# Macaron block on one core: KAN sums on four strips of the array instead of two, with another order of the start

## The chip, the cores and the metric

One core of a Trainium2 chip runs the whole program; the other cores are idle. The metric is the device time of one execution in microseconds, as the median of several runs. Shorter is better.

## The reference

Sixteen sequences (rows, below) of 512 tokens with 128 features pass through six residual steps; the first three concern the change.

```python
x = x + 0.5 * _L0_ffn_ref(_layernorm(x, axis=-1), ...)   # the KAN
x = x + _L0_attn_ref(_layernorm(x, axis=-1), ...)        # causal attention, 16 heads of 8, 4 key heads, RoPE
x = x + 0.5 * _L0_ffn_ref(_layernorm(x, axis=-1), ...)   # the same KAN again
x = x + 0.5 * _L1_ffn_ref(...)                           # 8 experts, each takes its best 128 tokens of a row
x = x + _L1_attn_ref(...)                                # gated linear recurrence
x = x + 0.5 * _L1_ffn_ref(...)                           # the experts again
```

The KAN maps 128 features to 64 scalars, gives each scalar 16 hidden ReLU units of its own, sums them with weights to 64 scalars again, and maps these to 128 features:

```python
s = jnp.einsum('btd,dm->btm', x, Win) + bin_         # 64 scalars
h = jax.nn.relu(s[..., None] * W1 + b1)              # 64 x 16
g = jnp.einsum('btmh,mh->btm', h, W2) + b2           # 64
out = jnp.einsum('btm,md->btd', g, Wout) + bout
```

## The kernel before, in words

All 16 rows of x stay in SBUF (`x[b]`, 128 x 4 x 128). The program is written as Python generators. Each runs one small piece of work up to a `yield`; `turn()` steps every open generator once, first those in `urgent`, then those in `sides`. What stands in the instruction queues of the engines is the order in which these pieces were stepped when the program was built. Nothing reorders it on the chip, apart from the waits.

**Rows.** From the main loop at the end, each row of attention takes 44 turns. In a turn `weights(b)` (L590 on) makes one bank of transposed scores on PE (L608, 72 + 27 = 99 partitions of `kp` and `qp`, bf16), its exponential on ACT (L611, into `pt`) and the causal mask of the diagonal block on POOL (L613). In the same turn `maxima(b + 1)` makes one bank of scores of the next row on PE (L550; a mask through L546) and its maximum on DVE (L555, L560). Both kinds of banks are double-buffered in PSUM. After a quarter of a row, `outputs` multiplies `pt` with the values (L631, four heads on four 32-column strips), transposes (L642) and divides (L646, L647). `max_rows` turns half a row's maxima into extra rows of `qp` (L581 transposes, L585 copies into `mr`, then DMAs on SP).

**Side work.** During rows from b = 0 on a budget per turn (`MOST`: pe 1.5, dve 1.15, act 0.85, pool 1.45) spreads the other work: a generator that says `yield from need(pe=1.0)` waits for a turn with that much room. The side work is: `norm` (L257 and L261 statistics on DVE, L263 and L264 on POOL, L278 on DVE, transposes L288 on PE, copy L292 on ACT); `kan(b)`, twice per row, before and after attention; `attn_in(b)`, the projections and rotation of a later row; `stage_out`, `gated`, `routing`.

**kan(b).** One fp32 matmul (L303) makes the 64 scalars twice, on partitions 0 to 63 and 64 to 127; ACT copies them to `kan_s` (L307). `kan_held` lets one KAN at a time use the accumulator `ps_kg`. Then, over 15 turns, ACT makes eight activations (L329), each with two hidden units per scalar, into four rotating buffers `kan_h`. After every second one, a pair of matmuls (L335, 128 x 64 weights `w2d`, 512 columns) adds to `ps_kg`: the first into partitions 0 to 63, the second into 64 to 127. ACT copies the sum (L340), PE applies `wout` (L346, doubled over both halves), DVE adds to x (L349). A constant is added to x on POOL (L332).

**attn_in(b).** The rotated queries `ta` and keys `ka` are split into three bf16 parts by `parts`: cast on ACT (L356), subtract on POOL (L359), cast on ACT (L362), subtract on POOL (L365). `spread` writes each part to DRAM on SP's queue, from where DMAs load `kp` (L434) and `qp` (L442) with the parts repeated.

**The start.** Constants are loaded on ACT's queue (L123 to L134) and SP's (L147 on), x on SP's. `center_win` folds the mean into `win`. Row 0's first pieces are stepped, then `prepare()` (L457 on: `rbias`, `kcst`, `w2d`, folded `wq`, `wk`, `wv`, masks, memsets of ten `QP` on POOL at L493 and of three `KP` on DVE at L495 and L496, `gateT`), with row 0 after it in each turn. Then rows 1 and 2. Row 0's maxima fill 44 turns of their own before the paced rows. After the rows comes the expert stage with the recurrence.

Of the kernel before, what the change touches and what calls it, by code (L numbers as in the profile page):

```python
# [8 lines left out]
F32 = mybir.dt.float32  # L9
# [7 lines left out]
P = 128  # L17
S = 512
NT = S // P
D = 128  # L20
M = 64
HALF = 8
HD = 8
# [21 lines left out]
def tile_macaron(  # L45
# [51 lines left out]
    with ExitStack() as ph:  # L97
# [4 lines left out]
        vap = ph.enter_context(tc.tile_pool(name="p1_va", bufs=4))  # L102
        hp = ph.enter_context(tc.tile_pool(name="p1_h", bufs=4))
        ptp = ph.enter_context(tc.tile_pool(name="p1_pt", bufs=2))
# [12 lines left out]
        nc.vector.tensor_scalar_add(center, ident, -1.0 / D)  # L117
        win = cst.tile([D, 2, M], F32, name="win")
        binc = cst.tile([P, 1], F32, name="binc")
        kw1 = cst.tile([P, HALF], F32, name="kw1")  # L120
        kb1 = cst.tile([P, HALF], F32, name="kb1")
        kw2 = cst.tile([P, HALF], F32, name="kw2")
        nc.scalar.dma_start(out=win, in_=win_in.unsqueeze(1).to_broadcast([D, 2, M]))  # L123
        nc.scalar.dma_start(out=kw1, in_=kw1_in.rearrange("m (a h) -> a m h", a=2))
        nc.scalar.dma_start(out=binc, in_=bin_in.unsqueeze(0).to_broadcast([2, M]))
        nc.scalar.dma_start(out=kb1, in_=kb1_in.rearrange("m (a h) -> a m h", a=2))
        nc.scalar.dma_start(out=kw2, in_=kw2_in.rearrange("m (a h) -> a m h", a=2))
        kb2 = cst.tile([M, 1], F32, name="kb2")
        nc.scalar.dma_start(out=kb2, in_=kb2_in.unsqueeze(1))
        wout = cst.tile([P, D], F32, name="wout")  # L130
        nc.scalar.dma_start(out=wout, in_=wout_in.unsqueeze(0).to_broadcast([2, M, D]))
        bout = cst.tile([1, D], F32, name="bout")
        nc.scalar.dma_start(out=bout, in_=bout_in.unsqueeze(0))
        nc.scalar.dma_start(out=gate_sb, in_=gate_in)  # L134
        rbias = cst.tile([P, HALF], F32, name="rbias")

        w2d = cst.tile([P, HALF, M], F32, name="w2d")
        eye2 = cst.tile([P, M], F32, name="eye2")
        ones = cst.tile([1, P], F32, name="ones1")
# [14 lines left out]
        rope = cst.tile([P, 2, S], F32, name="rope")  # L154
        nc.sync.dma_start(out=rope, in_=rope_in)
        for b in range(1, B):
            load(b)
# [64 lines left out]
        def bank(shape, dtype, name, work=0.0):  # L222


            while held[0] == 2 or (paced[0] and work > room["pe"]):
                yield
            room["pe"] -= work
            held[0] += 1
            return mm.tile(shape, dtype, name=name, tag="mm")

        def freed():
            held[0] -= 1
# [66 lines left out]
        def kan(b):  # L299

            _, xT = yield from norm(x[b])
            ps = yield from bank([P, S], F32, "ps_s", 0.9)
            nc.tensor.matmul(ps, lhsT=win.rearrange("d a m -> d (a m)"), rhs=xT, start=True, stop=True)  # L303
            yield
            sk = w2p.tile([P, S], F32, name="kan_s")
            take(act=0.6)
            nc.scalar.copy(sk, ps)  # L307
            freed()
            yield
            while kan_held[0]:  # L310
                yield
            kan_held[0] = 1

            pg = kap.tile([P, S], F32, name="ps_kg")
            hs = []
            begin = now[0]
            for t in range(HALF + 1):
                while now[0] < begin + 15 * t // 8:
                    yield
                pair = t % 2 == 0 and t > 0  # L320
                work = {"act": 0.8} if t < HALF else {}
                if pair:
                    work["pe"] = 1.0
                if t == 1:
                    work["pool"] = 1.25
                yield from need(**work)
                if t < HALF:
                    h = hp.tile([P, S], F32, name="kan_h")
                    nc.scalar.activation(h, sk, AF.Relu, bias=rbias[:, t : t + 1], scale=kw1[:, t : t + 1])  # L329
                    hs.append(h)  # L330
                if t == 1:
                    nc.gpsimd.tensor_tensor(x[b], x[b], kcst.unsqueeze(1).to_broadcast([P, NT, D]), ALU.add)  # L332
                if pair:
                    for i in range(2):
                        nc.tensor.matmul(pg[i * M : (i + 1) * M, :], lhsT=w2d[:, t - 2 + i, :], rhs=hs[t - 2 + i],  # L335
                                         start=(t == 2), stop=(t == HALF))
                yield
            gT = hp.tile([P, S], F32, name="kan_h")
            take(act=0.6)
            nc.scalar.copy(gT, pg)  # L340
            kan_held[0] = 0
            kans[0] -= 1
            yield
            po = yield from bank([P, NT, D], F32, "ps_ko", 0.9)
            for c in range(NT):
                nc.tensor.matmul(po[:, c, :], lhsT=gT[:, bass.ts(c, P)], rhs=wout, start=True, stop=True)  # L346
            yield
            take(dve=0.7)
            nc.vector.tensor_add(x[b], po, x[b])  # L349
            freed()  # L350
            yield

        def parts(r, dst, copies, **work):

            yield from need(**work)
            copies(dst[:, 0, :], r)  # L356
            yield
            yield from need(pool=1.15)
            nc.gpsimd.tensor_tensor(r, r, dst[:, 0, :], ALU.subtract)  # L359
            yield  # L360
            yield from need(**work)
            copies(dst[:, 1, :], r)  # L362
            yield
            yield from need(pool=1.3)
            nc.gpsimd.tensor_tensor(dst[:, 2, :], r, dst[:, 1, :], ALU.subtract)  # L365
            yield
# [8 lines left out]
        def attn_in(b, st):  # L375
# [45 lines left out]
            def keys():  # L421
                yield from need(pool=1.25)
                nc.gpsimd.tensor_tensor(ka, ka, kb, ALU.add)
                yield
                yield from parts(ka, kpart, nc.scalar.copy, act=0.6)

# [25 lines left out]
        def center_win():  # L452
            psc = yield from bank([P, 2 * M], F32, "ps_kc0")
            centered(psc, win.rearrange("d a m -> d (a m)"))
            freed()

        def prepare():  # L457

            nc.vector.scalar_tensor_tensor(rbias, in0=kw1, scalar=binc, in1=kb1, op0=ALU.mult, op1=ALU.add)
            nc.gpsimd.memset(ones, 1.0)  # L460
            nc.gpsimd.memset(onec, 1.0)
            psc = yield from bank([1, D], F32, "ps_kc")
            nc.tensor.matmul(psc, lhsT=kb2, rhs=wout[0:M, :], start=True, stop=True)
            nc.vector.tensor_add(kcr, psc, bout)
            freed()
            yield

# [3 lines left out]
            freed()  # L471
            nc.vector.tensor_add(eye2, ident[:, 0:M], ident[:, M:P])
            for u in range(HALF):
                nc.vector.tensor_scalar(w2d[:, u, :], eye2, kw2[:, u : u + 1], 0.5, ALU.mult, ALU.mult)
                if u == HALF // 2:
                    yield
            yield
# [9 lines left out]
            nc.vector.tensor_copy(wk[:, 1, :, hh:HD], wk[:, 0, :, 0:hh])  # L487
            make_identity(nc, identb)
            nc.gpsimd.memset(causal[:, 0 : S - P], 0.0)
            make_causal_mask(nc, own, NEG)  # L490
            yield
            for i in range(NQP):
                nc.gpsimd.memset(QP[i][MXR - 32 : MXR, :, :], 0.0)  # L493
                if i < NKP:
                    nc.vector.memset(KP[i][MXR - 32 : MXR, :, :], 0.0)  # L495
                    nc.vector.memset(KP[i][MXR : MXR + 3, :, :], 1.0)  # L496
                yield
            psg = yield from bank([D, E], F32, "ps_gate")
            nc.tensor.transpose(psg, gate_sb, ident[0:E, 0:E])
            nc.vector.tensor_copy(gateT, psg)  # L500
            freed()
            yield

# [60 lines left out]
        def max_rows(b, half, maxs):  # L564
# [17 lines left out]
            yield  # L582
            mr = w2p.tile([3 * H2, S], BF16, name="mr")
            take(dve=0.4)
# [337 lines left out]
        def folded():  # L922


            tmp = w2p.tile([P, 2, M, 4], F32, name="wu", tag="kan_s")
            wu, wvb = tmp[:, 0, :, :], tmp[:, 1, :, :]
# [40 lines left out]
        def recurrence(pair):  # L967
# [8 lines left out]
            yield  # L976
            fg = w2p.tile([P, S], F32, name="fg", tag="kan_s")
            nc.scalar.activation(fg, pf, AF.Tanh, scale=0.5)
# [58 lines left out]
        def finish(*gs):  # L1037
# [3 lines left out]
            paced[0] = pace  # L1041

        run(center_win())
        first = stage_in(0, sts[0])
        for _ in range(8):
            step(first)
        sides.append(prepare())
        sides.append(first)
        for _ in range(12):
            turn()  # L1050
# [98 lines left out]
```

## Time and profile before

| what | value |
|---|---|
| median of 3 runs | 1758.36 us (1757.0 to 1758.48) |
| profiled execution, its own time | 1763.15 us |
| its span | 1761.4 us |
| mean granted PE clock | 0.968 |
| PE busy | 1636.1 us (93%) |
| DVE busy | 1106.0 us (63%) |
| ACT busy | 996.6 us (57%) |
| POOL busy | 996.6 us (57%) |
| stages by time | start to 76 us, row 0's maxima to 128 us, rows to about 1010 us, experts to the end |

A line of a timeline has its start in us, its length in us, the engine, the line of the kernel, the operation, what it writes and reads, partitions and elements, the count, and in brackets how long the engine sat idle before it and what ended that. PEld are weight loads, which run beside matmuls. An fp32 matmul leaves two records. A wait line reads: who waited, for whom, us in total, times, longest.

### The profile page before, as it was taken

The page shows a single profiled execution, that of the slowest core. Times are in us where ns is not written, and L with a number is a line of the kernel's source. Part 1 is how long each engine was busy: PE and PEld are TensorE (multiplying, and loading weights), DVE is VectorE, ACT ScalarE, POOL GpSimd, SP SyncE. Part 2 cuts the span into 40 slices and gives each one's busy share as a digit, 9 for nine tenths or more (in the row PEclk, how much of TensorE's full clock was granted, in tenths as well). Part 3 has the DMA queues.
Part 4 walks back from the last instruction along what each step waited for, and adds up shares of the span by engine and source line. Part 5 has one row for each costly group of instructions (what it writes and reads, how often), then busy time and mean ns, then how long its engine had stood idle before and what let it go on. Part 6 is the DMA issues. An engine that isn't in the chain of part 4 may idle for free. (4 is left out here: it accounts for less than half of the span.)

```text
span 1761.4 us, 35249 instructions
## 1 busy us (share of the span) xinstructions
PE 1636.1 (93%) x12879; PEld 1110.9 (63%) x12879; DVE 1106.0 (63%) x3594; ACT 996.6 (57%) x2000; POOL 996.6 (57%) x1463
## 2 busy tenths in 40 slices
PE   3688999999999999999989899999999999999996
PEld 2234444444444454444444389799988889999996
DVE  5477767777777788878877137734458444672222
ACT  2435667787777776776666654344443334444443
POOL 5524445455554555455434767577663677647773
PEclk8879989999999999999999899999998999999998
DMA  4110111011101111011022113233322233323342
GB/s 116 57 66 26 50 47 30 35 48 54 42 31 40 51 54 38 21 50 50 25 71 68 32 43 70 49 73 65 66 59 45 58 67 71 68 52 69 65 81 47
DMA packets 101753, 94.77 MB, mean 54 GB/s; under 512 B 11859, under 2 KB 90140, under 8 KB 101340
## 3 DMA queue, kind: packets, MB, share of 16 engines
q1 hardware_dynamic: 74512, 67.45, 12.4%
q0 software_dynamic: 26048, 24.93, 8.8%
q8 instruction: 101, 1.65, 0.4%
q14 instruction: 72, 0.59, 0.1%
q10 hardware_dynamic: 1020, 0.15, 0.0%
HBM read 58.93 MB, written 37.49 MB: 55 GB/s over the span
## 5 line engine op out<-in xcount | busy, mean ns | idle before, releaser
L611 ACT ACTIVATE pt<-ps_st 128x512 f32<-128x512 f32 (+1 forms) x704 | 386.9, 561 | 242.3 <-PE ps_st L608 236.9
L613 POOL TENSOR_SCALAR_AFFINE_SELECT pt<-pt 128x128 f32<-128x128 f32 (+2 forms) x704 | 246.9, 355 | 409.1 <-ACT pt L611 404.3
L555 DVE CUSTOM_DVE_ANT_0 below<-ps_sc,causal 128x512 bf16<-128x512 f32 (+1 forms) x512 | 316.3, 618 | 120.8 <-PE ps_sc L550 106.6
L867 ACT ACTIVATE mo<-ps_h 128x512 f32<-128x512 f32 x256 | 153.1, 598 | 260.9 <-PE ps_h L865 260.7
L791 POOL DMA_INDIRECT xg<-xnd,tokI x256 | 250.1, 977 | 79.4 <-issue 42.8
L865 PE MATMUL ps_h<-xin,mw 128*128 128x128 f32 x2048 | 279.2, 279 | 0.0
L880 PE MATMUL ps_y<-mw,mo 128*128 128x128 f32 x2048 | 273.7, 277 | 0.0
L550 PE MATMUL ps_sc<-kp,qp 72*128 72x512 bf16 (+3 forms) x1024 | 261.4, 308 | 10.2 <-DVE maxs L555 7.5
L608 PE MATMUL ps_st<-qp,kp 99*128 99x512 bf16 (+3 forms) x1024 | 261.0, 308 | 5.6 <-ACT pt L611 4.6
L912 POOL DMA_INDIRECT sum<-ye,tokI x124 | 201.8, 1628 | 100.9 <-issue 25.3
L865 PEld LDWEIGHTS ps_h<-xin,mw 128*128 128x128 f32 x2048 | 250.5, 192 | 6.4 <-issue 3.7
L880 PEld LDWEIGHTS ps_y<-mw,mo 128*128 128x128 f32 x2048 | 251.0, 193 | 2.2 <-issue 0.8
L608 PEld LDWEIGHTS <-kp 99*128 99x128 bf16 x1024 | 94.3, 101 | 204.5 <-issue 186.3
L329 ACT ACTIVATE kan_h<-kan_s,rbias,kw 128x512 f32<-128x512 f32 x256 | 206.5, 814 | 7.6 <-PE ps_kg L335 7.3
L560 DVE TENSOR_REDUCE maxs<-ps_sc 128x2 f32<-128x512 f32 (+1 forms) x192 | 130.5, 685 | 69.2 <-PE ps_sc L550 68.2
L631 PE MATMUL ps_av<-pt,va 128*32 128x512 f32 (+3 forms) x2048 | 166.8, 444 | 0.0
L335 PE MATMUL ps_kg<-kan_h,w2d 128*64 128x512 f32 x512 | 164.2, 639 | 2.2 <-ACT kan_h L329 2.2
L550 PEld LDWEIGHTS <-qp 72*128 72x128 bf16 x1024 | 97.6, 101 | 56.0 <-issue 33.8
L886 DVE TENSOR_TENSOR mo<-mo 128x128 bf16<-128x128 f32 x132 | 38.9, 295 | 137.7 <-ACT mo L871 137.5
L898 PE MATMUL acc<-mo 128*128 128x128 bf16 x1584 | 112.4, 219 | 6.3 <-DVE mo L886 6.2
L898 PEld LDWEIGHTS <-mo 128*128 128x128 bf16 x1584 | 98.9, 98 | 24.1 <-issue 22.9
L631 PEld LDWEIGHTS ps_av<-pt,va 128*32 128x32 f32 x2048 | 53.6, 109 | 92.7 <-issue 49.1
(195 smaller groups left out, 2333.3 us busy)
## 6 DMA issues: line engine op xcount, KB each, us to landing
qp<-qs SPq DMA_DIRECT2D x64, 288.0 KB
xnd<-kan_x SPq DMA_DIRECT2D x32, 256.0 KB
sum<-x SPq DMA_DIRECT2D x31, 256.0 KB
qs<-qpart SPq DMA_DIRECT2D x48, 128.0 KB
kp<-ks SPq DMA_DIRECT2D x48, 96.0 KB
x<-in_L_attn_x_dram SPq DMA_DIRECT2D x16, 256.0 KB
mw<-in_L_ffn_w_dram SPq DMA_DIRECT2D x16, 256.0 KB
xg<-xnd,tokI POOLq DMA_INDIRECT x256, 2.5
```

The lines of the kernel that those rows point to most:

```text
L329: nc.scalar.activation(h, sk, AF.Relu, bias=rbias[:, t : t + 1], scale=kw1[:, t : t + 1])
L550: nc.tensor.matmul(v[:, u, 0:n], lhsT=qp[r][0 : 9 * HD, g, bass.ts(c, P)], rhs=kp[0 : 9 * HD, r, 0:n], start=alone, stop=(u == len(gs) - 1 ...
L555: nc.vector.tensor_tensor_reduce(below[:, 0:n], v[:, 0, 0:n], causal[:, S - n : S], 1.0, LOWEST, ALU.add, ALU.max, accum_out=maxs[:, c, h ...
L608: nc.tensor.matmul(v[:, u, 0:n], lhsT=kp[ROWS, r, bass.ts(c, P)], rhs=qp[r][ROWS, g, c * P : S], start=True, stop=True)
L611: nc.scalar.activation(o, v[:, :, 0:n], AF.Exp, scale=HD ** -0.5)
L613: nc.gpsimd.affine_select(out=dg, in_=dg, compare_op=ALU.is_ge, fill=0.0, base=0, pattern=[[0, len(gs)], [1, P]], channel_multiplier=-1)
L631: nc.tensor.matmul(po[32 * g : 32 * g + 32, c * P : S], lhsT=va[:, c, r, :], rhs=pt[:, g, OFF[c] : OFF[c] + n], start=(c == 0), stop=(c == ...
L791: nc.gpsimd.indirect_dma_start(out=xgs[i // E % 2][:, i % E, :], out_offset=None, in_=xnd[b], in_offset=bass.IndirectOffsetOnAxis(ap=tokI[ ...
L865: nc.tensor.matmul(pst[:, f, :], lhsT=mw1[e][:, bass.ts(f, P)], rhs=xins[i // E % 2][:, i % E, :], start=True, stop=True)
L880: nc.tensor.matmul(py, lhsT=hs[u][:, f, :], rhs=mw2[e][:, f, :], start=(f == 0), stop=(f == NF - 1))
L898: nc.tensor.matmul(acc[:, c, :], lhsT=sels[u][:, bass.ts(c, P)], rhs=yes[u][:, w, :], start=(e == 0 and c == 0 and w == 0), stop=(e == las ...
L912: nc.gpsimd.indirect_dma_start(out=sums[k, b], out_offset=bass.IndirectOffsetOnAxis(ap=tokI[g][:, n : n + 1], axis=0), in_=ye[:, b % 2 * ( ...
```

## The change

1. `kan`: the 64 scalars are made in two halves of 32, each four times over (partitions 0 to 127), by two input matmuls and two copies, `kan_s0` and `kan_s1`; the second half is made once the accumulator is granted. Each of the eight activations has four hidden units for 32 scalars. After the fourth and the eighth, four matmuls (128 x 32 weights) add to four strips of 32 partitions of `ps_kg`. `kan_h` has five buffers.
2. Constants: `win`, `binc`, `kb2` and `wout` go on SP's queue, the last two after `rope`; `kw1`, `kb1`, `kw2` stay on ACT's. Each comes in two halves. `wout` is ordered as the strips are.
3. The start: row 0 is stepped ahead of `prepare`, `w2d` is made before the `kcst` matmuls, KP[0] and QP[0] are cleared before `win` is centered, all these memsets are on DVE, three more `QP` in `prepare`, the others 16 turns later with two turns between; there are 14 turns instead of 12 before row 1.
4. `parts`: the second part is written by a subtraction on POOL directly in bf16, and the cast on ACT goes.
5. Keys: two more turns between the sum on POOL and the first cast.
6. `mr` moves to the pool with one buffer.

```diff
-        hp = ph.enter_context(tc.tile_pool(name="p1_h", bufs=4))
+        hp = ph.enter_context(tc.tile_pool(name="p1_h", bufs=5))
...
+            sk = []
+            for half in range(2):
+                while half and kan_held[0]:
+                    yield
+                kan_held[0] |= half
+                ps = yield from bank([P, S], F32, "ps_s", 0.9)
+                nc.tensor.matmul(ps, lhsT=win[:, half, :, :].rearrange("d i m -> d (i m)"), rhs=xT,
+                                 start=True, stop=True)
+                yield
+                sh = (w1p if half else w2p).tile([P, S], F32, name=f"kan_s{half}")
+                take(act=0.6)
+                nc.scalar.copy(sh, ps)
...
-                pair = t % 2 == 0 and t > 0
+                four = t in (U // 2, U)
...
+                if four:
+                    for half, v, h in hs:
+                        o = half * M + v % 2 * MH
+                        nc.tensor.matmul(pg[o : o + MH, :], lhsT=w2d[:, half, v, :], rhs=h,
+                                         start=(t < U), stop=(t == U))
+                    hs = []
+                if t < U:
+                    half, v = t // 2 % 2, t // 4 * 2 + t % 2
                     h = hp.tile([P, S], F32, name="kan_h")
-                    nc.scalar.activation(h, sk, AF.Relu, bias=rbias[:, t : t + 1], scale=kw1[:, t : t + 1])
+                    nc.scalar.activation(h, sk[half], AF.Relu, bias=rbias[:, half, v : v + 1],
+                                         scale=kw1[:, half, v : v + 1])
...
-                if pair:
-                    for i in range(2):
-                        nc.tensor.matmul(pg[i * M : (i + 1) * M, :], lhsT=w2d[:, t - 2 + i, :], rhs=hs[t - 2 + i],
-                                         start=(t == 2), stop=(t == HALF))
...
             yield from need(pool=1.15)
+            nc.gpsimd.tensor_tensor(dst[:, 1, :], r, dst[:, 0, :], ALU.subtract)
+            yield
+            yield from need(pool=1.15)
             nc.gpsimd.tensor_tensor(r, r, dst[:, 0, :], ALU.subtract)
-            yield
-            yield from need(**work)
-            copies(dst[:, 1, :], r)
...
                 nc.gpsimd.tensor_tensor(ka, ka, kb, ALU.add)
+                yield
+                yield
                 yield
...
+        def cleared(pack):
+
+            nc.vector.memset(pack[MXR - 32 : MXR, :, :], 0.0)
+
+        def keys_cleared(i):
+
+            cleared(KP[i])
+            nc.vector.memset(KP[i][MXR : MXR + 3, :, :], 1.0)
...
-            for i in range(NQP):
-                nc.gpsimd.memset(QP[i][MXR - 32 : MXR, :, :], 0.0)
-                if i < NKP:
-                    nc.vector.memset(KP[i][MXR - 32 : MXR, :, :], 0.0)
-                    nc.vector.memset(KP[i][MXR : MXR + 3, :, :], 1.0)
-                yield
...
+            for i in range(1, NR):
+                cleared(QP[i])
+                yield
+            for _ in range(16):
+                yield
+            for i in range(NR, NQP):
+                if i - NR < NKP - 1:
+                    keys_cleared(i - NR + 1)
+                yield
+                yield
+                cleared(QP[i])
...
-            mr = w2p.tile([3 * H2, S], BF16, name="mr")
+            mr = w1p.tile([3 * H2, S], BF16, name="mr")
...
+        keys_cleared(0)
+        cleared(QP[0])
         run(center_win())
         first = stage_in(0, sts[0])
         for _ in range(8):
             step(first)
+        sides.append(first)
         sides.append(prepare())
-        sides.append(first)
-        for _ in range(12):
+        for _ in range(14):
             turn()
```

## The prediction

> **What bounds the kernel now.** I read the stage table first (windows of 200 us, each engine's busy time), then PE's timeline inside one window, then the waits of PE there, and last the timeline of the first 75 us. The page's chain of waits names only one POOL step at the very end, so it says nothing on what sets the pace.
>
> Columns of the stage table: busy us (instructions) of PE, PEld, DVE, ACT, POOL, granted clock, DMA share, GB/s.
>
> ```profile
> 400.00:600.00 200.00, 196.49 (x1416) 96.46 (x1415) 155.08 (x514) 151.65 (x278) 110.56 (x226) 1.00 0.14 47
> 600.00:800.00 200.00, 189.92 (x1344) 94.31 (x1343) 163.74 (x533) 142.08 (x261) 101.30 (x210) 0.97 0.11 37
> ```
>
> PE is 95 to 98% busy, DVE 78 to 82%, ACT 71 to 76%, POOL 51 to 55%. Busy PE alone proves little, so here is the timeline (start, length, instruction):
>
> ```profile
> 504.36 1.08 PE L335 MATMUL ps_kg<-kan_h,w2d 128*64 128x512 f32 x4
> 505.37 0.34 PE L608 MATMUL ps_st<-qp,kp 99*128 99x384 bf16 x1
> 505.55 0.33 PE L550 MATMUL ps_sc<-kp,qp 72*128 72x384 bf16 x1
> 505.71 1.02 PE L384 MATMUL ps_pa<-kan_xT,wq 128*128 128x512 f32 x2
> 506.57 0.38 PE L608 MATMUL ps_st<-qp,kp 99*128 99x256 bf16 x2
> ...
> 512.79 0.39 PE L608 MATMUL ps_st<-qp,kp 99*128 99x512 bf16 x1
> 513.01 0.38 PE L550 MATMUL ps_sc<-kp,qp 72*128 72x512 bf16 x1
> 513.32 1.06 PE L631 MATMUL ps_av<-pt,va 128*32 128x512 f32 x8
> 514.32 0.39 PE L608 MATMUL ps_st<-qp,kp 99*128 99x512 bf16 x1
> ```
>
> Each instruction starts before the record of the one before has ended; start to start is the true price. And PE's list of waits in this window is two lines, 3.6 us of 200:
>
> ```profile
> PE ps_s L303 <- ACT kan_xT L292: 2.9, 4, 0.7
> PE ps_o L658 <- ACT yT L292: 0.7, 4, 0.2
> ```
>
> So in the rows PE is the limit: the passes of ps_m (L581, two per row) stand 28.7 and 26.9 us apart, 55.6 us per row, repeating to 0.01 us from 320 to 627 us. From 600 to 1000 us PE waits some more (DVE y, rope_kb and va; about a tenth of the time). The expert stage after 1010 us has no KAN but the last row's.
>
> The start is different, a chain of waits:
>
> ```profile
> 15.96 16.16 POOL L493 MEMSET qp<- 32x2048 bf16 x9
> 19.82 1.72 DVE L450 COPY wq<-ps_kc 128x128 f32<-128x128 f32 x1
> 25.39 0.91 DVE L495 MEMSET kp<- 32x1024 uint32 x1 [0.25 <-issue]
> 26.79 1.76 DVE L496 MEMSET kp<- 3x2048 bf16 x1 [0.48 <-issue]
> 29.50 0.58 ACT L340 COPY kan_h<-ps_kg 128x512 f32<-128x512 f32 x1 [1.16 <-PE ps_kg L335]
> 35.40 1.64 DVE L257 BATCH_NORM_STATS2 ln_st<-x 128x6 f32<-128x128 f32 x8
> 39.63 1.11 PE L288 MATMUL ps_t<-ident,kan_x 128*128 128x128 f32 x4 [10.17 <-DVE kan_x L278]
> 42.16 1.92 PE L346 MATMUL ps_ko<-wout,kan_h 128*128 128x128 f32 x8
> ```
>
> Row 0's KAN is summed at 30.1, but its output matmul starts at 42.2: ahead of it on PE stand the transposes of rows 1 and 2, which wait for norms that stand on DVE behind three pairs of KP memsets. The first score matmul (L550) starts at 76.1.
>
> **What the Trainium skill says.** TensorEngine Tiling (Array Packing), Key Properties: tiles work in parallel, and a change of tiling mode drains the engine. The trace agrees: four strips (L631, 128x512, eight records) take 1.00 us start to start, two strips (L335) 1.01, one full matmul (L384) 0.86; the score matmul ahead of a strip group lasts 0.31 instead of 0.22, so a group costs 1.10 with its entry. Perfetto Trace Analysis, Identifying the Most-Contended Engine: matmul busy share is no measure of nearness to the limit; hence the start-to-start reading. SBUF — State Buffer, Who interferes with whom: GpSimd and some DVE copies share one port, and the later one blocks; the copy of wq under POOL's memsets took 1.72 us, the equally large copy of win (L450, at 5.00) 0.29. DMA: Bandwidth & Descriptors, Specifications: pieces under 512 B miss line rate; win's pieces shrink from 256 to 128 B, and before it landed by 4.20.
>
> **The change, part by part.** Own time of the profiled execution: 1763.15 us (span 1761.4, 1.75 around it), 0.27% above the median 1758.36; I subtract from it and carry the difference to the median.
>
> *KAN on four strips, PE.* Before, one KAN is one input matmul (0.86) and four pair groups: 0.86 + 4 x 1.10 = 5.26 us. After, two input matmuls and two groups of four: 2 x 0.86 + 2 x 1.10 = 3.92. Saved 1.34 us. Counted by L335's mean start to start (1.145, which contains waits) it is 1.50. A group of four 32-wide outputs of 128x512 f32 is just L631's form, so its price is seen, with one difference: in L631 the four moving tiles are slices of one pt.
>
> *Where it counts.* Of 32 KANs, 27 lie in the paced rows by the turns of the program as built (16 second ones, and the first ones of rows 5 to 15). 27 x 1.34 = 36.2 us of PE. With PE at 95 to 98% most becomes time; the later windows give back less. I take 95% for 18 KANs (22.9) and 75% for 9 (9.0): **-32 us**. Bounds: half of it, -18; all at 1.50, -40.
>
> *ACT.* Per KAN one copy more (L307, 580 ns); per part one cast less (L362, 617 ns). Two KANs and two parts a row: +1.16 - 1.23, nothing.
>
> *POOL.* Each part now takes three subtractions instead of two: 2 x 1.15 = 2.3 us a row, 37 us in all. POOL is 51 to 55% busy and becomes about 57. Behind each subtraction stand the masks of pt (L613, 306 ns), for which the weight loads of L631 wait (27.7 us in all, 60 times) while PE is still streaming. I take zero; if the cover failed each time, +37.
>
> *Keys two turns later, the second cast gone.* ACT waited 12.6 us for POOL before kpart's casts in 200 to 1000 us and 7.8 before qpart's; the second cast's waits (9.9) and most of the first kpart's (7.5) go. ACT is not the limit: zero. Row 5's parts end four turns later (some 5 us); its scores begin 32 turns after that, so the SP loads behind (qs, ks, kp, qp) keep some 40 us. Without that cover a late kp would stop PE by those 5 us a row.
>
> *Turns.* The built program has 44 turns in every row before and after, no overrun in either, and 789 in the expert stage; the fill has 68 instead of 63. A KAN holds the accumulator 16 to 20 turns before and some 20 after, since the input's second half now falls under its grant; two fit into 44. Five kan_h buffers cover the fifth activation while the group of four is pending. mr in one buffer waits for a DMA issued 27 us before: zero.
>
> *The start.* Losses: three memsets on DVE (0.91, 1.76, 0.91 and gaps) now stand ahead of win's copy, about +2 us; a second input matmul (2.04 at the cold clock). Gain: that matmul no longer stands behind the one that waits for wout (xT was ready at 10.3, ps_s started at 14.7). So the activations begin near 17.6 against 17.4, and the sum is ready near 27.5 against 30.1. DVE now has three QP memsets (3 x 1.4) before the norms of rows 1 and 2 instead of three KP pairs (10.0), and POOL none instead of 16.2: I put the output matmul at 33.5 against 42.2. A KP pair then stands in row 0's second norm (+3.4), and further memsets in its rotation (+2). Constants: win and binc go to SP ahead of wq (four issues of about 0.5), wout behind rope, wanted 10 us later; zero, at worst +3. First scores: **-7** (between +3 and -18). Between 76 and 128 us the clock is low (a pair group at 120.9 takes 1.9): two KANs save 2 us each, while DVE's maxima set much of the pace; I count half, **-2**.
>
> Sum: -32 - 7 - 2 = -41; 1763.15 - 41 = 1722, on the median **1717**.
>
> **Rivals.**
> A. PE's relief is absorbed: with PE lighter, each row is paced by the DVE and ACT round trips of the two-buffer score tiles. For: DVE is at 78 to 82%, and PE's waits are on DVE after 600 us. Against: 3.6 us of waits in 200. Only the start and a tenth of the rows' gain remain: 1758 - 9 - 4 = 1745.
> B. POOL late: every added subtraction lands before a mask that L631 needs: +37 on -41, 1754.
> C. The slower one: the four strips don't overlap, because four separate kan_h tiles stream at once. Then a group costs 4 x 0.86 + 0.24 = 3.68, a KAN 2 x 3.68 + 1.72 = 9.08, +3.82, times 27 = +103, less 9 at the start: 1852. It decides above 1.77 us a group. Against: L631 at 1.00.
> D. More than forecast: PE's waits shrink too and the start gives its bound: -40 - 22, 1696.
>
> **How the numbers follow.** Forecast 0.68 (own range 1700 to 1738, from -18 - 2 to -40 - 18), A 0.13, B 0.06, C 0.06, D 0.07. The range takes in A and most of D: 1692 to 1748. Measurement tells 0.2% (3.5 us) from no change. Faster: forecast, A, D and a third of B, 0.90; same, most of B, 0.04; slower, C, 0.06.
>
> **What would show it.** Right: ps_kg groups of eight records at 1.0 us start to start, two per KAN; the ps_m passes 53 us per row instead of 55.6; PE's waits in 400 to 600 us under 10; row 0's ps_ko near 33, first ps_sc near 69; POOL near 57%. Wrong: rows still at 55 with new PE waits on DVE or ACT (A); PE idle on pt's masks at L631 (B); ps_kg groups over 1.8 us (C); first scores later than 76.

## The result and the profile after

| | before | after |
|---|---|---|
| median on one chip | 1757.88 us (1757.0 to 1758.48, 4 runs) | 1780.78 us (1776.99 to 1784.3, 4 runs) |
| ratio, with its 95% interval | 1 | 1.0126 [1.0101, 1.015] |
| profiled execution, its span | 1761.4 us | 1776.6 us |
| mean granted PE clock | 0.968 | 0.954 |
| first score matmul (ps_sc) | 76.1 us | 72.7 us |
| first transposed scores (ps_st): the rows begin | 127.6 us | 125.3 us |
| last ps_st: the rows end | 1011.2 us | 1019.6 us |
| first matmul of the experts (ps_h) | 1018.1 us | 1030.3 us |
| rows, first to last ps_st | 883.6 us | 894.3 us |

The kernel is 1.3% slower where a gain of 41 us was forecast. By stages the span's +15.2 us are: start and fill -2.3, rows (from the first to the last ps_st) +10.7, rows to experts +3.8, experts +3.0. The medians differ by 22.9 us; the other 7.7 us lie between the profiled executions and the medians, and no stage can be named for them.

The stage table of the kernel after has the columns of the one before (PE, PEld, DVE, ACT, POOL, clock, DMA share, GB/s):

```profile
400.00:600.00 200.00, 185.88 (x1430) 93.05 (x1423) 152.64 (x505) 148.13 (x273) 116.70 (x228) 1.00 0.14 47
600.00:800.00 200.00, 180.78 (x1281) 90.09 (x1279) 156.49 (x499) 135.01 (x249) 104.50 (x205) 0.94 0.11 36
```

PE's busy time fell by 10.6 us in the first of these windows, as the four strips promised. But nothing was bought with it: the window holds 1% more PE records than before, which is no more than the new input matmuls add to each row, and the next one holds 5% fewer. PE's waits in 400 to 600 us, two lines and 3.6 us before, are now 12.5 us:

```profile
PE ps_s L329 <- ACT kan_s L334: 3.3, 4, 0.8
PE ps_t L309 <- DVE rden L697: 3.0, 4, 0.8
PE ps_t L309 <- DVE y L698: 2.9, 4, 0.7
PE ps_oq L693 <- ACT kan_xT L313: 2.2, 4, 0.6
PE ps_st L659 <- ACT pt L662: 1.1, 3, 0.4
```

Each line but the last comes four times, that is about once in each row. This points to single instructions that stand too early in PE's queue, not to an engine that is short of time; with a good part of ACT's work left out (e6 below) the first line stays as it is, 3.3 us in four waits. PE's timeline shows three of them within 5 us:

```profile
460.20 0.66 PE L693 MATMUL ps_oq<-ident,oT 128*128 128x128 f32 x4 [0.56 <-ACT kan_xT L313]
...
461.25 1.02 PE L329 MATMUL ps_s<-kan_xT,win 128*128 128x512 f32 x2
463.00 0.63 PE L309 MATMUL ps_t<-ident,y 128*128 128x128 f32 x4 [0.72 <-DVE y L698]
...
463.79 0.38 PE L601 MATMUL ps_sc<-kp,qp 72*128 72x256 bf16 x2
465.01 1.13 PE L329 MATMUL ps_s<-kan_xT,win 128*128 128x512 f32 x2 [0.83 <-ACT kan_s L334]
```

The last line is the KAN's second input matmul. In `kan`, no fixed `yield` stands between the copy of half 0 and the request for half 1's bank. The banks of `mm` (two, shared by all side work) come round in turn, so where another piece has taken the other one, half 1 gets the bank that the copy of this very turn has still to empty. The Trainium skill, PSUM — Partial Sum Buffer, Engine vs sequencer instructions, says that matmuls start and complete in program order; the trace agrees: the score matmuls behind L329, which need none of it, start only after it, and 0.83 us pass with PE idle.

So rows of 56.0 us came out (passes of ps_m, L632) where 55.6 stood before and 53 was forecast. Up to the pass at 596 us nothing is lost (470.8 us from the first ps_st; before, 471.1 to the pass at 598.7). Then one row takes 69.2 us, from 653.7 to 722.9; before, that row took 57.6. The stage table inside it shows what kind of loss it is:

```profile
682.00:690.00 8.00, 5.90 (x53) 3.63 (x46) 4.92 (x14) 3.01 (x7) 2.42 (x5) 0.89 0.09 25
690.00:700.00 10.00, 7.68 (x42) 5.15 (x41) 5.54 (x15) 3.73 (x7) 6.39 (x10) 0.75 0.10 26
700.00:710.00 10.00, 8.22 (x63) 3.79 (x61) 8.23 (x23) 7.57 (x15) 7.80 (x14) 1.00 0.18 60
710.00:723.00 13.00, 11.88 (x54) 5.06 (x55) 7.91 (x30) 6.29 (x11) 4.13 (x10) 0.61 0.23 79
```

The row has twelve waits of PE, 9.6 us in all (3.0 us in that row before), and two stretches at half the clock. Ahead of the first, POOL does nothing but masks from 684 us on. PE waits for `rope_kb`, which stands on DVE behind maxima, a norm and a piece of the routing, and from 689 to 695 us the clock is 0.50:

```profile
688.38 2.05 PE L376 MATMUL ps_ko<-wout,kan_h 128*128 128x128 f32 x8 [2.10 <-DVE rope_kb L437]
```

In the last line of the table PE is busy for 91% of the time at a granted clock of 0.61. The timeline just ahead of that second stretch, cut to four records of DVE and POOL and two of PE:

```profile
706.24 1.44 DVE L295 TENSOR_SCALAR kan_x<-x,ln_mv,ln_rstd 128x128 f32<-128x128 f32 x2
706.41 1.18 POOL L392 TENSOR_TENSOR rope_ka<-rope_ka,kpart 32x512 f32<-32x512 f32 x1
...
707.81 1.15 POOL L395 TENSOR_TENSOR kpart<-rope_ka,kpart 32x512 bf16<-32x512 f32 x1
...
708.08 2.46 DVE L295 TENSOR_SCALAR kan_x<-x,ln_mv,ln_rstd 128x128 f32<-128x128 f32 x2
708.21 0.32 PE L601 MATMUL ps_sc<-kp,qp 72*128 72x384 bf16 x1 [0.77 <-DVE maxs L606]
...
709.39 0.33 PE L309 MATMUL ps_t<-ident,kan_x 128*128 128x128 f32 x1 [0.64 <-DVE kan_x L295]
```

While POOL subtracts (and, from 709.2 us, adds the KAN's constant), two pairs of DVE's multiplications take 1.44 and 2.46 us; the mean of one multiplication over 320 to 627 us is 0.36 us. It is the kind of interference that the prediction quoted for the copy of `wq`, now in the rows. PE waits four times for DVE from 707.4 to 712.3 us, 2.8 us in all, and from 712.5 to 722.4 us its matmuls take twice their time. That the waits brought the low clock is read from their order in time, not tried. The Trainium skill, TensorE: Matmul & The Clock Gate, What's actually happening, has it that the clock is set by how busy PE was of late, and halved after an idle window of some 3.4 us; here no single wait ahead of the drop was longer than 0.9 us, with PE running in between, so this trace shows a drop without a whole idle window.

### The profile page after: what moved, and what is told of

It reads as the page before. It is cut to its first block, busy times and chain, and to the rows that moved or that the text cites. A ratio compares the mean times of both kernels' runs of the same rounds, so it can differ in the third digit from the quotient of the medians.

```text
span 1776.6 us, 35431 instructions
## 1 busy us (share of the span) xinstructions
PE 1620.0 (91%) x12943; PEld 1111.6 (63%) x12943; DVE 1118.8 (63%) x3606; ACT 993.0 (56%) x2000; POOL 1015.9 (57%) x1486
## 3 DMA queue, kind: packets, MB, share of 16 engines
q1 hardware_dynamic: 76060, 67.65, 12.5%
## 5 line engine op out<-in xcount | busy, mean ns | idle before, releaser
L659 PE MATMUL ps_st<-qp,kp 99*128 99x512 bf16 (+3 forms) x1024 | 262.4, 309 | 14.6 <-ACT pt L662 12.5
L916 PEld LDWEIGHTS ps_h<-xin,mw 128*128 128x128 f32 x2048 | 254.1, 195 | 6.3 <-issue 3.7
L611 DVE TENSOR_REDUCE maxs<-ps_sc 128x2 f32<-128x512 f32 (+1 forms) x192 | 130.8, 685 | 76.1 <-PE ps_sc L601 74.9
L285 POOL TENSOR_TENSOR ln_rstd<-ln_rstd,mhalf 128x4 f32<-128x4 f32 x96 | 100.7, 1049 | 8.0
```

The costliest lines, as they stand in the source:

```text
L659: nc.tensor.matmul(v[:, u, 0:n], lhsT=kp[ROWS, r, bass.ts(c, P)], rhs=qp[r][ROWS, g, c * P : S], start=True, stop=True)
L916: nc.tensor.matmul(pst[:, f, :], lhsT=mw1[e][:, bass.ts(f, P)], rhs=xins[i // E % 2][:, i % E, :], start=True, stop=True)
```

## The experiments

The runs were made on several chips. Before itself took 1798 us on the chip of the first four, 1846 us with the next four, 1761 us with e8 to e11, 1843 and 1849 us with the last two sets; it is the part after some 1,000 us that is longer there (span less last ps_st: 757 us in the kernel after, 832 us in its repetition). So ratios are within one chip, and stages are compared only up to the last ps_st, where the same kernel repeats (894.3 and 894.4 us for the rows of the kernel after).

### The parts of the change, each alone

`e1_kan` is before with `kan`, its constants and `mr` as in after (items 1 and 6, and the halves of item 2), `e2_parts` before with items 4 and 5 of the change, `e3_start` before with the new start. `e4_s1own` is after with half 1's input matmul in the accumulator's own bank:

```diff
-                ps = yield from bank([P, S], F32, "ps_s", 0.9)
+                if half:
+                    yield from need(pe=0.9)
+                    ps = kap.tile([P, S], F32, name="ps_s1", tag="ps_kg")
+                else:
+                    ps = yield from bank([P, S], F32, "ps_s", 0.9)
...
```

> The kernel before with the KAN change alone (two input matmuls, groups of four, five kan_h buffers, constants in halves on ACT's queue, mr in one buffer); start, parts and keys as before. Theory 1: the KAN change itself is the loss, since its second input matmul takes one more turn of the two shared mm banks and PE, with less work, waits for copies and then loses clock: rows 55.5 to 56.5 us, total 1765 to 1785. Rival 2 (the three subtractions on POOL are the loss): this one is faster, 1720 to 1745. Rival 3 (the start's new order is the loss): the same, 1720 to 1745.

> The kernel before with the parts and keys change alone (second part by a subtraction on POOL, keys' cast two turns later). Theory 1: no loss here, 1750 to 1762. Rival 2: most of the 23 us are here, 1772 to 1785, with PE waiting behind POOL.

> The kernel before with the new start alone (loads on two queues, row 0 ahead of the preparation, memsets on DVE and spread, 14 turns). Theory 1: the first scores come 3 to 10 us earlier and little of it is lost, 1748 to 1760. Rival 3: 1770 to 1785, with clock lost or waits shifted in the later rows.

> The changed kernel with one edit: the second input matmul of a KAN goes to the KAN's own accumulator bank, which is idle then, and no longer to the two shared mm banks. Theory 1: the waits on kan_s, y and rden vanish, rows 53 to 54.5 us instead of 56.0, total 1735 to 1760. If the shared banks are not the cause: 56 us per row, 1775 to 1785.

| | ratio | first ps_sc | first ps_st | rows |
|---|---|---|---|---|
| e1_kan | 1.0086 [1.0053, 1.0119] | 88.6 | 136.4 | 882.7 |
| e2_parts | 1.0198 [1.0164, 1.0233] | 83.3 | 133.6 | 909.3 |
| e3_start | 0.9926 [0.9902, 0.995] | 64.2 | 116.6 | 882.5 |
| e4_s1own | 1.0023 [1.0004, 1.0041] | 73.3 | 126.0 | 880.9 |

Three things follow. The KAN alone gains 0.9 us in the rows instead of 32: the relief is absorbed without any help from the parts. (e1 is late from its start: 12.5 us at the first scores, 8.8 at the first ps_st. Its constants, about twice as many loads, stayed on ACT's queue there; that they are the reason was not tried.) The parts, priced at nothing, lose 25.7 us in the rows. The start alone is worth more than forecast, -11.9 us to the first scores.

In e4 the wait of ps_s on kan_s went, and others came. PE's waits of e4 in 200 to 1000 us:

```profile
PE ps_sc L606 <- DVE maxs L616: 13.2, 20, 0.9
PE ps_st L664 <- ACT pt L667: 9.2, 28, 0.9
PE ps_t L309 <- DVE y L703: 8.1, 10, 1.8
PE ps_s L333 <- ACT kan_h L375: 7.1, 8, 0.9
```

Rows now take 57.1 and 55.5 us in turn, 56.3 on average against 56.0. The rows' total fell by 13 us mostly because the row of 69.2 us was not there (58.3 in its place). That the shared banks alone cost the relief, the first theory, is not what this run shows; neither forecast for it came true.

In e2, DVE's multiplications show the port. Before and e2, each in 320 to 627 us (count | busy us, mean ns of one):

```profile
L274 DVE TENSOR_SCALAR kan_x<-x,ln_mv,ln_rstd 128x128 f32<-128x128 f32 x20 | 7.5, 418 | 0.0
```

```profile
L274 DVE TENSOR_SCALAR kan_x<-x,ln_mv,ln_rstd 128x128 f32<-128x128 f32 x20 | 22.4, 1162 | 0.0
```

PE's waits on `maxs`, which stand behind them on DVE, are 21.1 us in 200 to 1000 us of e2, against 3.2 before.

The traces of all runs agree on when such a multiplication is slow. In 200 to 1000 us, 313 of them had no POOL instruction beside them, and none of these took more than 349 ns; each of the 150 that took over 500 ns had one. But it need not be an added subtraction: in e1, whose POOL work is that of before, the mean over 320 to 627 us is 593 ns, with the KAN's constant (L366) and masks beside the slow ones. So the order decides which instructions meet.

### Is it the engines' time?

`after_again` repeats the kernel after. `e5_less_pe` is before without one of the four pair groups of each KAN. `e6_after_act` and `e7_before_act` leave out every second activation of the KAN, in after and before.

```diff
-                if pair:
+                if pair and t != 4:
```

```diff
-                    h = hp.tile([P, S], F32, name="kan_h")
...
+                    if t % 2 == 0:
+                        h = hp.tile([P, S], F32, name="kan_h")
...
```

> The changed kernel once more, on the same chip as the three below. If its loss is the mechanism of the program and not of one execution: ratio 1.010 to 1.015 again, rows of 56.0 us to row 10 and one row near 69 us after 680 us. If the row of 69 us was an accident of that execution: no such row, ratio 1.003 to 1.008.

> The kernel before without the second of the four pair groups of every KAN (a quarter of the KAN's sum is left out): 1.10 us less PE work per KAN and nothing else. Theory P (PE sets the pace of the rows): rows of 53.4 instead of 55.6 us, total 30 us less. Theory Q (PE is only just in front; ACT's and DVE's copies come next): rows of 55 to 55.6 us, less than 8 us in total.

> The changed kernel with four of the eight activations of each KAN left out, each hidden tile used twice (ACT has 3.3 us less per KAN). Theory Q with ACT next in line: rows fall from 56.0 to 52 to 54 us, PE's waits on kan_s, kan_xT and pt go. Theory P, or DVE next in line: 55 to 56 us.

> The kernel before with four of the eight activations of each KAN left out, each hidden tile used twice. Theory P: PE is the limit, rows stay within 0.3 us of 55.6. Theory Q: under 55 us.

| | ratio | row, 320 to 600 us | rows |
|---|---|---|---|
| after_again | 1.0141 [1.0109, 1.0172] | 56.0, then again one of 69.2 | 894.4 |
| e5_less_pe | 0.9885 [0.9796, 0.9975] | 54.6 | 872.3 |
| e6_after_act | 1.006 [1.0009, 1.0111] | 56.0 | 890.6 |
| e7_before_act | 0.9972 [0.9945, 0.9998] | 54.4 | 869.1 |

Taking 2 x 1.10 = 2.2 us of PE out of a row of before shortens it by 1.0: 45%, not 95%, and between the two forecasts. Taking eight activations of 0.81 us, 6.5 us of ACT, out of a row shortens before by 1.2 us, which theory P had excluded, and after by nothing; the long row of after stays too (67.9 us). ACT's time does not set the rows of after, and its long row is no accident of one execution.

e7 also shows what the list of waits in before had left out. Two pair groups of before, one after the other, and what the second one waits for:

```profile
376.66 1.08 PE L335 MATMUL ps_kg<-kan_h,w2d 128*64 128x512 f32 x4
...
382.51 2.02 PE L335 MATMUL ps_kg<-kan_h,w2d 128*64 128x512 f32 x4
382.59 0.81 ACT L329 ACTIVATE kan_h<-kan_s,rbias,kw 128x512 f32<-128x512 f32 x1
...
383.45 0.19 PEld L335 LDWEIGHTS ps_kg<-kan_h,w2d 128*64 128x64 f32 x2 [0.75 <-ACT kan_h L329]
```

The pair's second matmul starts only when its activation has ended on ACT, at 383.4 us. The records of the group overlap, so all of the time counts as busy, and the wait is listed for the weight loads alone (PEld), not for PE. From 321 to 599 us of before, 30 of the 40 groups take 1.0 us start to start, and 10, two in each row, take 1.64 or 1.95; in e7 all 40 take 1.0. So PE waited for ACT for 1.6 us a row that its own list does not have. In e5 these waits are 0.5 us a row longer, a part of what its gain lacks.

### Old parts, and the second half later

`e8_old_parts` is after with the parts and the keys' cast of before; `e9_half_later` is after with the two lines below; `e10_both` has both edits; `e11_parts_only` is before with item 4 alone.

```diff
+                for _ in range(2 * half):
+                    yield
                 while half and kan_held[0]:
```

> The kernel after, with the old parts (ACT makes the second cast, two subtractions of POOL a part) and the keys' cast at its old place; the four-strip KAN and the start stay. Theory P (the added subtractions collide with DVE's copies at certain moments, and the row of 69 us is such a moment): that row is gone or under 62, the rows from first to last ps_st take about 883 us as in KAN alone instead of 894, and the ratio falls from 1.013 to 1.000 to 1.004. Rival (the long row is KAN's and the start's doing): the row of about 69 us stays, rows about 890, ratio 1.009 to 1.013.

> The kernel after, with two turns more between the first half's ACT copy and the second half's input matmul. Theory Q (the second half's matmul, put in the turn of the copy that frees its bank, stops PE each time): the waits of ps_s on kan_s go from 3.3 us in 200 to below 0.5 and the row from 56.0 to about 55.2; with all four waits linked, down to 54. Rival (the order of PE's work and its few shared banks only hand the wait on to the next instruction): ps_s no longer waits, another wait of 2 to 4 us in 200 takes its place, row 55.7 to 56.5.

> Both edits: old parts and keys' cast, and the second half's input matmul two turns later, in the kernel after. If the losses are separate and add up (P and Q): rows about 872 to 878 and a ratio of 0.992 to 0.998, better than before. If the waits are only handed on: rows 880 to 885, ratio 1.000 to 1.004.

> The kernel before with three subtractions of POOL and one cast of ACT a part, the keys' cast at its old place (KAN, start and the two turns as before). Theory P (the subtraction makes the loss of parts and keys together, 1.020): DVE's kan_x multiplications of 128x128 take about 1.0 us instead of 0.42, rows about 900 to 910 us instead of 884, ratio 1.012 to 1.020. Rival (the keys' two turns move the work to a bad moment): kan_x stays near 0.45, rows about 884 to 888, ratio 1.000 to 1.005.

| | ratio | row, 320 to 600 us | rows |
|---|---|---|---|
| e8_old_parts | 1.0014 [1.0005, 1.0023] | 57.3 and 55.8 | 881.8 |
| e9_half_later | 1.0443 [1.0404, 1.0481] | 54.1 at first, then 58 to 71 | 951.2 |
| e10_both | 1.0011 [1.0, 1.0022] | 54.6 | 881.5 |
| e11_parts_only | 1.0073 [1.0052, 1.0094] | 57.6 | 889.2 |

The second theory (P) was that POOL's subtractions hold DVE up at the port. e8 has the times that P expects, but not for P's reason: its kan_x takes 595 ns on average in 320 to 627 us, and that of after 362. e9 fits no theory: two turns added to one wait, and the rows take 57 us more (its granted clock is 0.91 in 400 to 600 us and in 600 to 800 us, where after has 1.00 and 0.94). With the old parts (e10) the same two turns give rows of 54.6 us, the shortest so far with all the work done, but the rows before and after that stretch give the gain back. And e11 goes against P: rows are 2 us longer, while kan_x takes 386 ns, less than before. Its waits are others, and most of them are on ACT. The three longest of PE in 320 to 627 us:

```profile
PE ps_ko L346 <- ACT kan_xT L292: 7.0, 5, 1.4
PE ps_s L303 <- ACT yT L292: 4.2, 5, 0.8
PE ps_pb L390 <- DVE y L647: 2.8, 5, 0.6
```

Before has in the same stretch:

```profile
PE ps_s L303 <- ACT kan_xT L292: 3.6, 5, 0.7
PE ps_o L658 <- ACT yT L292: 0.8, 5, 0.2
```

Five times each, once in a row: the order on PE has become another. The two programs as built say so too: PE's instructions are the same in both, none added, but they stand in another order. What wrote it anew is the planner: `need(act=0.6)` became `need(pool=1.15)`, so that this step, and then others, found room in other turns.

### Order and work apart

Third theory (O): the loss comes from the order that the charges write. `e12_old_turns` is before with the three subtractions, the third step charged as the cast was. As built, its instructions on PE and on DVE are those of before in the same order. `e13_new_turns` is the reverse: before's own two subtractions and two casts, the second cast charged to POOL. Its instructions on PE and DVE are those of e11 in the same order. `e14_after_old_turns` and `e15_later_old_turns` give that step the cast's charge in after and in e9, by this edit:

```diff
             nc.gpsimd.tensor_tensor(dst[:, 1, :], r, dst[:, 0, :], ALU.subtract)
             yield
-            yield from need(pool=1.15)
+            yield from need(**work)
             nc.gpsimd.tensor_tensor(r, r, dst[:, 0, :], ALU.subtract)
```

> The kernel before with three subtractions of POOL and one cast a part, but the third step keeps the charge of the cast (act=0.6) in the planner, so PE and DVE do their instructions in the very order of the kernel before; only the engine of one step of a part changes. Theory O (the parts' loss comes from the order that the planner's charges write, not from POOL's work): row 55.6 us, rows about 884, ratio 0.999 to 1.002. Rival P (POOL's added work holds DVE up or comes late): row 56.5 to 57.6, ratio 1.005 to 1.01, with kan_x or the masks longer.

> The reverse: the kernel before with its own cast on ACT and its two subtractions, but the cast is charged to POOL (pool=1.15) in the planner, so PE and DVE do their instructions in the order of the run with three subtractions; no work is added. Theory O: row 57.6 us as there, rows about 889, ratio 1.005 to 1.009. Rival P: row 55.6, ratio 0.999 to 1.002.

> The kernel after with three subtractions a part, the third step charged as the cast was (act=0.6), the keys' two turns as in after. Theory O: the row of 69 us goes and the ratio comes near the 1.0014 of old parts in the kernel after (1.000 to 1.005). Rival P: the ratio stays at 1.010 to 1.014 and a row of over 65 us remains.

> The kernel after with the second half's input matmul two turns later (1.044 alone, rows of 60 to 71 us) and the third step of a part charged as the cast was. Theory O: the rows of over 65 us go and the ratio falls to 0.999 to 1.006, near the 1.0011 with old parts and keys. Rival P: rows of over 65 us remain, ratio 1.03 to 1.045.

| | ratio | row, 320 to 600 us | rows |
|---|---|---|---|
| e12_old_turns: work without order | 1.0123 [1.0046, 1.0201] | 56.4 | 894.5 |
| e13_new_turns: order without work | 1.0059 [1.0027, 1.009] | 57.7 | 889.4 |
| e14_after_old_turns | 0.9921 [0.989, 0.9952] | 54.9 | 863.7 |
| e15_later_old_turns | 0.9976 [0.9939, 1.0013] | 55.9, at most 59.3 | 884.2 |

e13 shows that order alone costs 5.8 us in the rows with nothing added, as much as e11 (5.6 us): there O holds, and P is out. But e12 refutes O as the only cause. In the very order of before, the subtractions cost 10.9 us: 0.8 us in each row from 320 to 600 us (kan_x 512 ns instead of 418, two new waits of PE, on pt 3.6 us and on y 2.5 us in 320 to 627 us), 3.9 us in the second row (52.4 instead of 48.5), 3.0 us after 600 us. The two do not add up either: e11 has both and loses 5.6.

e14 is the plainest. It does the same work as after; one charge in the planner is another; and the rows are 30.6 us shorter. PE's instructions are again the same in another order. Its row at the place of the 69.2 takes 56.7 us. e15 against e9 is the same step: 67 us. (The profile of e15 is of an execution of 1858.0 us, over its median of 1844.0; the ratios, 1.0443 and 0.9976, show the step as well.)

What the order changes can be split. PE idle is the rows less PE's busy time there. Lost to the clock is an estimate: the rows times what their mean granted clock lacks to 1 (0.974 before, 0.964 after, 0.984 in e14). The rest is then PE at full speed.

| us | rows | PE idle | lost to the clock | rest |
|---|---|---|---|---|
| before | 883.6 | 46.1 | 23.2 | 814.3 |
| e13_new_turns | 889.4 | 64.4 | 6.0 | 819.0 |
| e1_kan | 882.7 | 77.8 | 27.3 | 777.6 |
| e8_old_parts | 881.8 | 76.4 | 27.3 | 778.1 |
| after | 894.3 | 80.1 | 32.3 | 781.9 |
| e14_after_old_turns | 863.7 | 73.5 | 13.6 | 776.6 |
| e9_half_later | 951.2 | 104.2 | 73.6 | 773.4 |

The rest of before and of e13, which have the same instructions, differs by 5 us, so the split is good to about that. With the new KAN the rest falls by some 32 to 41 us, about as forecast (36.2), though a part of it is the waits inside the pair groups. PE's idle time grows by 27 to 34 us and takes most of that back (58 us in e9). Between after and e14 the clock makes 19 of the 30.6 us and idle time 7. Waiting alone does not set the clock: in e13 PE is idle for 18 us more than before, and 17 us less are lost to the clock.

### The better version

`e14_again` repeats e14. `e17_ko_first` is e14 with `range(18)` for `range(14)` turns before row 1 is begun, so that row 0's output matmul stands ahead of the transposes of rows 1 and 2.

> The kernel after with three subtractions and the third step charged as the cast, once more and in more rounds. If the gain is the order's, as the run before it says: rows of 54.9 us, first to last ps_st about 864 us, ratio 0.985 to 0.996. If that ratio was an accident of a chip with a long expert stage: 0.997 to 1.005.

> The same with 18 turns instead of 14 before row 1 is begun, so that row 0's output matmul stands ahead of the transposes of rows 1 and 2 on PE. If the start lost its forecast by that order: ps_ko near 25.6 instead of 29.7, first scores at 66 to 70 instead of about 74, the rows as in the kernel it is made from, ratio 0.003 to 0.004 lower. Rival (memsets on DVE and the slow clock set the first row's chain): ps_ko earlier, first scores still at 72 to 76, ratio within 0.002 of it.

e14_again: 0.9922 [0.9888, 0.9956], rows 864.3, as before it. Stage table of e14_again:

```profile
400.00:600.00 200.00, 187.67 (x1461) 96.50 (x1459) 155.76 (x513) 151.02 (x281) 116.26 (x231) 1.00 0.14 47
600.00:800.00 200.00, 182.53 (x1384) 90.43 (x1381) 171.61 (x552) 144.41 (x268) 116.68 (x228) 1.00 0.12 38
```

PE is hardly busier than in after, but passes 2% and 8% more records of the same program in the same time, and the clock of the second window is 1.00 instead of 0.94.

e17_ko_first: 0.9879 [0.9832, 0.9926], the lowest ratio of the study. In e17, PE's start runs like this:

```profile
25.20 1.16 PE L376 MATMUL ps_ko<-wout,kan_h 128*128 128x128 f32 x8 [0.68 <-ACT kan_h L370]
27.82 1.12 PE L309 MATMUL ps_t<-ident,kan_x 128*128 128x128 f32 x4 [1.45 <-DVE kan_x L299]
29.52 1.09 PE L309 MATMUL ps_t<-ident,kan_x 128*128 128x128 f32 x4 [0.59 <-DVE kan_x L299]
```

In the kernel after:

```profile
24.62 0.59 ACT L370 COPY kan_h<-ps_kg 128x512 f32<-128x512 f32 x1 [1.14 <-PE ps_kg L356]
...
27.49 0.66 PE L309 MATMUL ps_t<-ident,kan_x 128*128 128x128 f32 x4 [2.91 <-DVE kan_x L299]
...
29.11 0.80 PE L309 MATMUL ps_t<-ident,kan_x 128*128 128x128 f32 x4 [0.96 <-DVE kan_x L299]
29.71 1.92 PE L376 MATMUL ps_ko<-wout,kan_h 128*128 128x128 f32 x8
```

The sum is ready at 25.2 in both; behind the two transposes the matmul comes 4.5 us later, and slower (1.92 us for 1.16; the granted clock is 0.58 from 29 to 32 us). First scores come at 66.7 us instead of 74.7 in e14_again. The rows take 871.0 instead of 864.3 us, against the forecast, so most of that is given back: 1.5 us are left at the last ps_st. The ratio is 0.004 lower, but the intervals of the two overlap.

## Why the prediction was wrong, by its own steps

- **Four strips on PE.** Right. Groups of eight records on ps_kg are 1.00 us start to start, and PE's work in the rows fell by an estimated 32 us (36.2 forecast). Rival C is out.
- **Where it counts (-32).** Wrong, and with the turns the step that failed most: the rows gained nothing by it. The term took 95% of PE's relief as time, because PE waited only 3.6 us of 200. That list lacked the waits inside the pair groups, 1.6 us a row. And a short list shows that the present order has few holes, not that a shorter instruction leaves none: of 2.2 us taken out in e5, 45% came through; in after PE's idle time in the rows rose from 46 to 80 us; in e1, with the KAN change and none of the parts, 0.9 us were gained. In e14 the rows are 19.9 us shorter than before's, close to -18, the lower bound named there. That is partly luck: 9.6 us of it are a better clock. And e8, with the same KAN, old parts and the keys not delayed, gains only 1.8 us, so the keys' two turns have a share in it that was not tried in before alone.
- **POOL (taken as zero).** Wrong, and not by the cover that was named. The weight loads of ps_av waited 21.9 us for the masks before and 23.3 after in 200 to 1000 us, and 26.5 and 40.8 us for all of POOL; but ps_av is not once in PE's list of waits there, and its 2,016 matmul records in the rows take 156 us in both, so the cover held and rival B's mechanism is out. The work showed on DVE instead. The prediction cited the shared port for one copy of the start and did not ask the same of 37 us of added subtractions, nor of the POOL work that a new order would move. In before's order the subtractions cost 10.9 us (e12).
- **Turns (equal).** Wrong, by as much. Both programs have 44 turns in every row, which was true and was read as "nothing moves". The charge of item 4 put the steps inside the rows into other turns: 5.8 us by itself in before (e13), 30.6 us between after and e14, 67 us between e9 and e15. With the new charge the kernel is 1.3% slower than before, with the old one 0.8% faster (e14).
- **Keys two turns later (zero).** Not settled alone: parts with the keys' delay lose 25.7 us in the rows (e2), without it 5.6 us (e11), and e14 has the delay and is fast. The delay adds no work, so it acts through the order too; before with the delay alone was not run.
- **Start (-7).** The sign was right, the size half: -3.4 us. The output matmul came at 29.7 (33.5 was forecast), but then time was lost: row 0's second norm stood among DVE's memsets, and the clock in 44 to 88 us fell from 0.85 to 0.74. Which of the two cost it was not tried. e17 shows the order of ps_ko as the lever on this stretch, e3 what the start gives with the old KAN (-11.9).
- **76 to 128 us (-2).** Not seen: the fill took 52.6 us instead of 51.5.
- **The end (not in the sum).** +3.8 us from the last ps_st to the experts. The last row's ps_ko starts 1.2 us after the last ps_st (1020.80), before it started 1.4 us ahead of it (1009.78). The experts' +3.0 us was not tried.

Rival A has the right kind (the relief was absorbed), but not its cause: the score tiles' round trips (ps_sc on maxs, ps_st on pt) are 16 of PE's 65 us of waits in 200 to 1000 us of after, and the longest of the others are single instructions in PE's queue, about once a row each. And it kept the old order as its floor, so it could not end above 1758. What stays open is why one order is better than another by 20 to 67 us, and above all why it keeps the clock; these runs show that it is the order, and what it changes in waits and clock, not a rule that would have told beforehand.

## What to carry to other kernels

In a program whose order is written by a planner, the charge of a step is a change of its own: keep the charge and change the work, then keep the work and change the charge, and compare the instruction listings of each engine before pricing anything. An engine that is always busy and has few waits need not return what is taken from it: 45% in the even rows where the order was kept (e5), 0.9 of some 36 us where it was not (e1). Compare equal groups of its instructions with each other, since a group that takes twice its time hides a wait. Price work that moves to POOL by what DVE does at that moment, not only by who waits for POOL.

## What was not expected of the hardware

- A 128 x 128 fp32 multiplication of DVE took 418 ns on average before and 1162 ns with POOL's subtractions beside it (e2), while in other orders with the three subtractions it took 386 (e11) or 343 ns (e14). Without a POOL instruction beside it, none of 313 took over 349 ns.
- Four waits of PE of 0.5 to 0.9 us within 4.9 us were followed by 10 us at half speed in the kernel after. That row paid twice; e13, with more waits than before and a better clock (0.993 for 0.974), shows that this is no rule.
